# Two-layer graph attention: the place of the shared slot tile among the gathers of layer 2

## The chip, the core and the metric

The kernel runs on one core of a Trainium2 chip. The metric is the device time of one execution, in microseconds. A core has five engines with instruction queues of their own: TensorE (PE), VectorE (DVE), ScalarE (ACT), GpSimd (POOL) and SyncE (SP). SP, ACT and POOL also issue transfers between the chip's memory (DRAM) and the core's buffers; these run on 16 DMA engines that all queues share.

## The reference

The input is a graph of 3125 nodes with 768 features each, and 53,125 edges sorted by target node: 25,000 pairs in both directions and a loop on every node. The reference normalizes and rectifies the features, and passes them through two layers of graph attention:

```python
def gat_conv(x, edge_index, W, a_src, a_dst, bias, heads, out_ch, concat):
    xl = (x @ W).reshape(n, heads, out_ch)
    e = leaky_relu(alpha_src[src] + alpha_dst[dst], 0.2)
    e = exp(e - segment_max(e, dst)[dst])
    alpha = e / (segment_sum(e, dst)[dst] + 1e-16)
    out = segment_sum(xl[src] * alpha[:, :, None], dst)
...
h = relu(layer_norm(gat_conv(x, ei, W1, ..., 4, 256, True), g1, be1)) + (h0 @ Wr1 + br1)
h1 = h
h = layer_norm(gat_conv(h, ei, W2, ..., 1, 768, False), g2, be2) + (h1 @ Wr2 + br2)
return x + h
```

Layer 1 has four heads of 256 columns, layer 2 one head of 768. For every edge, the row of the edge's source node has to be fetched, weighted, and added into the row of its target node. `edge_index` adds one more loop per node, which the kernel treats apart (`own`).

## The kernel before

**Tiles.** The nodes are cut into 25 node tiles: 24 of 128 nodes and a last one of 53. The edges that end in a node tile are laid into 17 *slot tiles* of 128 slots each (`J = 17`, L31; 8 for the last node tile). A slot is one edge. The slot tiles belong to the four quarters of the node tile, 32 nodes each (`QUARTERS`); slot tile 0 belongs to the first quarter and slot tile 16 to the last. The node tiles form chains of three (`CHAIN = 3`): 0, 1, 2; then 3, 4, 5; and so on. Within a chain, slot tile 16 of one node tile and slot tile 0 of the next are the same tile: it holds the overhang of the first and the beginning of the second, and is gathered once. `shared(b)` says that node tile `b` has its slot tile 0 from the tile before: it is true for 1, 2, 4, 5, 7, 8 and so on up to 23.

**Layer 2.** `table2` in DRAM has one row of 784 numbers per node: 768 features, then the source score in column 768. A *gather* (`gather`, L206) fetches for one slot tile the 128 rows of its source nodes, some 400 KB, by an indirect transfer that GpSimd issues. Lines L210 and L214 are its two forms. L214 is used for the last slot tile of a node tile (16, or 7 in the last node tile) from the 37th gather on; it leaves out slots that hold no edge. The gathers of the whole layer are 400.

**The ring.** The gathered rows lie in a ring of 36 buffers `g0` to `g35` (`RING`, L1237). `slots_due` (L1333) is the list of all gathers in their order: node tile after node tile, and within one the five `ROUNDS` (0, 5, 9, 13), (1, 6, 10, 14), (4, 11, 15), (2, 8, 16), (3, 7, 12), less slot tile 0 where it is shared. Gather number n uses buffer n modulo 36. `fetch` (L1338) asks for further gathers as long as they are less than 36 ahead of the first one in the list whose rows are still needed (`unused`). A shared slot tile is still needed until the first round of the next node tile: `summed` lets it go there (L1408, L1409). A node tile takes 17 gathers, or 16 where its slot tile 0 is shared: 49 for a chain of three.

**Who uses a gathered tile.** Two engines do. ScalarE copies its score column into `slots` (`values`, L1357, L1360). When all slot tiles of a node tile have been copied, `softmax` (L1371) transposes the scores on TensorE into `mix` (L1378), takes maximum and exponentials, and transposes the weights back (L1394). Then `summed` (L1401) multiplies weights and rows on TensorE, one round at a time, into `pa` (L1421). `finish` (L1426) normalizes the node tile and stores it.

**The order.** The order of the instructions on TensorE, VectorE and ScalarE is the order in which the code writes them (`manual_schedule`, L1465). The main loop (L1482) goes through the node tiles b and their rounds. Rounds are counted from one in this text. In the second round the loop writes, behind `summed` and the square root of the finish of the tile before, the copies of the fourth round (slot tiles 2, 8, 16) of node tile b + 1; in the third round the copies of its fifth round (slot tiles 3, 7, 12) and the first half of its softmax; the second half and the steps of the residual product `pr` (`residuals`, helper line L190) fill the rest. So node tile b cannot go past its third round before all slot tiles of node tile b + 1 have landed.

The order on GpSimd and SyncE is not written by hand. A planner sets it when the kernel is built: it takes the instructions in the order of the code, but lets one that it holds ready pass an earlier one that is still waiting. An instruction that stands in GpSimd's queue runs in that order, and a gather waits there until the previous user of its buffer is done.

Of the kernel before, what the change touches and what calls it, by code (L numbers as in the profile page):

```python
# [30 lines left out]
J = 17  # L31
S = J * 128
QUARTERS = [(0,), (0,), (0,), (0,), (0, 1), (1,), (1,), (1,), (1, 2), (2,), (2,), (2,), (2, 3), (3,), (3,), (3,), (3,)]
ROUNDS = [(0, 5, 9, 13), (1, 6, 10, 14), (4, 11, 15), (2, 8, 16), (3, 7, 12)]
# [9 lines left out]
@with_exitstack  # L44
def preln_gat2_kernel(
    ctx: ExitStack,
    tc: tile.TileContext,
    x, src, dst,
    W1, a_src1, a_dst1, b1, g1, be1, Wr1, br1,
    W2, a_src2, a_dst2, b2, g2, be2, Wr2, br2,  # L50
    out,
):

    pool = ctx.enter_context(tc.tile_pool(name="flag", bufs=1))
    flag = pool.tile([1, 1], I32, name="flag")  # L60
    in_order(tc, x, src, dst, W1, a_src1, a_dst1, b1, g1, be1, Wr1, br1,
             W2, a_src2, a_dst2, b2, g2, be2, Wr2, br2, out, flag)
    other = tc.nc.values_load(flag[0:1, 0:1], min_val=0, max_val=1)
    with tc.If(other > 0):
        any_order(tc, x, src, dst, W1, a_src1, a_dst1, b1, g1, be1, Wr1, br1,
                  W2, a_src2, a_dst2, b2, g2, be2, Wr2, br2, out)
# [3 lines left out]
def in_order(  # L70
# [23 lines left out]
    NB = -(-N // P)  # L94
# [28 lines left out]
    def shared(b):  # L123

        return b < NB - 1 and b % CHAIN > 0
# [4 lines left out]
    def tiles_of(b):  # L130
        return J if b < NB - 1 else JL
# [1100 lines left out]
    with tc.tile_pool(name="m2", bufs=1, reuse_waits="tile") as mp, \  # L1232
# [95 lines left out]
        def filled(n):  # L1328
            for _ in range(n):
                next(fill, None)  # L1330

        gs = {}
        slots_due = [(b, j) for b in range(NB) for k in ROUNDS for j in k  # L1333
                     if j < tiles_of(b) and not (j == 0 and shared(b))]
        order_of = {s: i for i, s in enumerate(slots_due)}
        asked, unused = 0, set(range(len(slots_due)))

# [658 lines left out]
```

## Time and profile before

| | us |
|---|---|
| three runs | 1757.60, 1760.58, 1760.94 |
| median | 1760.58 |
| the profiled execution | 1760.3 |
| its span, first to last instruction | 1758.5 |
| mean granted TensorE clock | 0.968 |

The profile is that of one execution. In its lines a group or an instruction is named by its line in the kernel, its engine, its operation and the tiles that it writes and reads (`g<-table,idx_s` is a gather of the form L210, `g<-table,hi_s` one of L214). In the chain of waits each line has start, length and what the time went to. In the timeline each line has start, busy time, instruction, and in brackets the idle time of the engine before it, with what ended it. The windows have, for each stretch, its length, the busy time (and count) of PE, PEld (the loading of weights), DVE, ACT and POOL, the granted clock, the mean busy share of the DMA engines and the GB/s that they moved. The DMA share can come out slightly over 1.

### The profile page before, as it was taken

How to read it: one execution, taken by the hardware profiler on the slowest of the kernel's cores; microseconds unless marked ns; L12 is line 12 of the kernel's file. 1: busy time of each engine (PE TensorE's matmuls, PEld its weight loads, DVE VectorE, ACT ScalarE, POOL GpSimd, SP SyncE). 2: the span in 40 equal slices, each digit the busy share in tenths (PEclk: the TensorE clock that was granted, in tenths of full speed). 3: DMA queues.
4: the chain of work that ended last, by engine and by line, in shares of the span. 5: the costliest groups of instructions: out<-in, count | busy, mean ns of one | idle time of the engine just before them, and what ended most of it. 6: DMA issues, size and time to landing. Idle time of an engine off the chain costs nothing.

```text
span 1758.5 us, 31362 instructions
## 1 busy us (share of the span) xinstructions
PE 1632.8 (93%) x11522; PEld 936.7 (53%) x11522; DVE 1005.1 (57%) x2604; ACT 457.3 (26%) x1312; POOL 872.0 (50%) x908
## 2 busy tenths in 40 slices
PE   7999999999989999999999999997988988988984
PEld 5666666566656556556556555544444443443431
DVE  7784343788864566556565566641444544544545
ACT  2222342000122112212122122122333433433432
POOL 2000012100055766667666667627767667667662
PEclk9999999899989999999999999998999999989987
DMA  7833546533189999999999999969999999999994
GB/s 241 280 120 110 147 129 208 233 132 129 37 313 369 409 400 404 393 403 409 404 393 406 375 374 387 399 228 373 373 370 395 370 359 396 371 357 392 364 328 156
DMA packets 188644, 546.69 MB, mean 311 GB/s; under 512 B 32120, under 2 KB 80632, under 8 KB 188354
## 3 DMA queue, kind: packets, MB, share of 16 engines
q0 software_dynamic: 99632, 386.94, 57.9%
q1 hardware_dynamic: 84456, 147.27, 23.9%
q10 hardware_dynamic: 4394, 10.39, 1.5%
q8 instruction: 94, 1.54, 0.4%
q14 instruction: 68, 0.56, 0.1%
HBM read 492.19 MB, written 65.62 MB: 317 GB/s over the span
## 4 chain that ended last, share of the span: by engine, by line
PE 76%; DMA 14%; DVE 5%; issue 2%; ACT 2%; POOL 1%; SPq 0%; POOLq 0%; DVEq 0%; ACTq 0%
PE pr L190 18%; PE p L190 13%; PE pm L190 12%; PE pa L775 11%; PE pm L1027 7%; PE pa L1421 6%; DMA g<-table,idx_s 5%; DMA g<-table,hi_s 4%; PE pq L580 3%; PE mix L1378 1%; DMA w<-in_L_gnn_W_dram 1%; PE p L1190 1%; DMA h<-h1T_d 1%; DMA s<-slo_d 1%; PE pt L859 1%
## 5 line engine op out<-in xcount | busy, mean ns | idle before, releaser
L210 POOL DMA_INDIRECT g<-table,idx_s x393 | 378.8, 964 | 358.4 <-PE pq L610 170.9
L214 POOL DMA_INDIRECT g<-table,hi_s x423 | 433.6, 1025 | 203.8 <-issue 85.3
L190 PE MATMUL pr<-wr,h 128*128 128x384 f32 x768 | 277.3, 507 | 2.9 <-issue 2.1
L190 PE MATMUL p<-w,h1T 128*128 128x384 f32 (+1 forms) x768 | 267.7, 496 | 0.0
L775 PE MATMUL pa<-g,w 128*32 128x256 f32 x3912 | 246.7, 386 | 8.3 <-DVE w L752 5.6
L190 PEld LDWEIGHTS pr<-wr,h 128*128 128x128 f32 x768 | 143.7, 197 | 112.8 <-issue 35.9
L190 PEld LDWEIGHTS p<-w,h1T 128*128 128x128 f32 x768 | 139.8, 189 | 113.0 <-issue 21.4
L775 PEld LDWEIGHTS pa<-g,w 128*32 128x32 f32 x3912 | 119.7, 110 | 128.3 <-issue 23.8
L1421 PE MATMUL pa<-g,w 128*32 128x384 f32 x1956 | 176.7, 499 | 2.6 <-DVE v L1455 2.6
L752 DVE TENSOR_TENSOR w<-oh,al 128x128 f32<-128x128 f32 (+1 forms) x416 | 132.3, 318 | 51.9 <-PE pa L775 27.2
L190 PE MATMUL pr<-h0k,wr 128*128 128x256 f32 (+1 forms) x576 | 143.0, 395 | 2.5 <-DMA h0k<-h0T_d 2.5
L1027 PE MATMUL pm<-h0g,wr 128*128 128x512 f32 x288 | 133.1, 609 | 0.0
L190 PE MATMUL pm<-w,h0g 128*128 128x344 f32 x432 | 131.5, 459 | 0.3 <-ACT h0g L861 0.3
L190 PE MATMUL pm<-w,h0l 128*128 128x344 f32 x432 | 129.5, 454 | 0.0
L190 PEld LDWEIGHTS pr<-h0k,wr 128*128 128x128 f32 x576 | 106.9, 192 | 32.7 <-issue 10.7
L958 POOL DMA_DIRECT2D hot_d<-ohd x25 | 13.4, 535 | 213.2 <-DVE own L531 123.6
L1421 PEld LDWEIGHTS pa<-g,w 128*32 128x32 f32 x1956 | 57.5, 111 | 113.1 <-issue 104.7
L751 DVE TENSOR_SCALAR oh<-iota_f,rel_s 128x32 f32<-128x32 f32 (+1 forms) x416 | 114.4, 275 | 3.7 <-issue 3.5
L190 PEld LDWEIGHTS pm<-w,h0g 128*128 128x128 f32 x432 | 81.6, 193 | 40.1 <-issue 1.4
L190 PEld LDWEIGHTS pm<-w,h0l 128*128 128x128 f32 x432 | 80.5, 190 | 39.1 <-issue 0.2
L1382 DVE CUSTOM_DVE_ANT_0 mix<-mix,pen 128x640 f32<-128x640 f32 x25 | 20.8, 832 | 129.7 <-PE mix L1378 129.7
L1223 DVE COPY asad<-p 128x2 f32<-128x2 f32 (+1 forms) x25 | 4.0, 159 | 155.3 <-ACT row L1221 155.3
(295 smaller groups left out, 1751.4 us busy)
## 6 DMA issues: line engine op xcount, KB each, us to landing
s<-slo_d SPq DMA_DIRECT2D x25, 544.0 KB
table<-row SPq DMA_DIRECT2D x24, 512.0 KB
own<-table SPq DMA_DIRECT2D x24, 512.0 KB
h1T_d<-h1T SPq DMA_DIRECT2D x24, 512.0 KB
h<-h1T_d SPq DMA_DIRECT2D x88, 128.0 KB
table<-row SPq DMA_DIRECT2D x24, 392.0 KB
ring<-in_x_dram SPq DMA_DIRECT2D x24, 384.0 KB
out_dram<-z ACTq DMA_DIRECT2D x24, 384.0 KB
```

What stands on the lines that cost most here:

```text
L190: nc.tensor.matmul(out_, lhsT, rhs, start=start, stop=stop)
L210: nc.gpsimd.indirect_dma_start(out=g, out_offset=None, in_=table[:, :], in_offset=bass.IndirectOffsetOnAxis(ap=idx_s[:, c], axis=0))
L214: nc.gpsimd.indirect_dma_start(out=g, out_offset=None, in_=table[:, :], in_offset=bass.IndirectOffsetOnAxis(ap=idx_k[:, c], axis=0), bound ...
L580: nc.tensor.matmul(q[:, j], oh[:P, o:o + 128], tabs[:, i], start=(i == 0), stop=(i == 2))
L751: nc.vector.tensor_scalar(oh, iota_f[:, lo:hi], rel_s[:, c:c + 1], None, op0=OP.is_equal)
L752: nc.vector.tensor_tensor(w, oh[:, None, :].to_broadcast([128, heads, hi - lo]), al[:, POS[j], :, b:b + 1].to_broadcast([128, heads, hi - ...
L775: nc.tensor.matmul(pa[p0:p0 + 32, o // f, o % f:o % f + n], w[:, o // cols, :], g[:, o:o + n], start=to not in opened, stop=False, skip_gr ...
L859: nc.tensor.transpose(pt[:, k, :r], xt[:, (k0 + k) * 128:(k0 + k + 1) * 128], ident[:r, :r])
L1027: nc.tensor.matmul(pm, wr1[:, k, m * 128:(m + 1) * 128], groups[gi][:, k, :], start=(k == 0), stop=(k == NK1 - 1))
L1190: nc.tensor.transpose(pt[:, k, :r], z[:, (k0 + k) * 128:(k0 + k + 1) * 128], ident[:r, :r])
L1382: nc.vector.tensor_tensor_reduce(out=sums_, in0=sums_, in1=pen, scale=1.0, scalar=-BIG, op0=OP.add, op1=OP.max, accum_out=top)
L1421: nc.tensor.matmul(pa[p0:p0 + 32, i, :f], w_, g[:, i * f:(i + 1) * f], start=(i, q) not in opened, stop=False, skip_group_check=True)
```

## The change

In a node tile whose slot tile 16 is shared with the next one, that slot tile goes to the end of the node tile's gathers, behind slot tiles 3, 7 and 12. It was among the gathers of the fourth round. The order in which the rows are used, the copies on ScalarE and the matmuls stay as they are, and so does the order of gathers in node tiles whose slot tile 16 is not shared (2, 5, 8 and so on, 23 and 24).

```diff
         gs = {}
-        slots_due = [(b, j) for b in range(NB) for k in ROUNDS for j in k
-                     if j < tiles_of(b) and not (j == 0 and shared(b))]
+
+        def due(b):
+
+            js = [j for k in ROUNDS for j in k if j < tiles_of(b) and not (j == 0 and shared(b))]
+            return sorted(js, key=lambda j: j == J - 1) if shared(b + 1) else js
+
+        slots_due = [(b, j) for b in range(NB) for j in due(b)]
         order_of = {s: i for i, s in enumerate(slots_due)}
         asked, unused = 0, set(range(len(slots_due)))
```

## The prediction

> **What bounds the kernel now.** I read the page first, then the chain of waits in order of time, then windows and the timeline of layer 2. The edit touches only layer 2, which runs from about 1190 us to the end.
>
> ```profile
> PE 1632.8 (93%) x11522; PEld 936.7 (53%) x11522; DVE 1005.1 (57%) x2604; ACT 457.3 (26%) x1312; POOL 872.0 (50%) x908
> ...
> DMA  7833546533189999999999999969999999999994
> ...
> PE 76%; DMA 14%; DVE 5%; issue 2%; ACT 2%; POOL 1%; SPq 0%; POOLq 0%; DVEq 0%; ACTq 0%
> ```
>
> TensorE sets most of the chain, but 14% of it are transfers. The chain in order of time (start, length, what) says where, and they come in step:
>
> ```profile
> 1235.15 2.77 PE pa L1421 x32
> ...
> 1240.83 0.70 PE mix L1378 x5
> ...
> 1254.02 2.72 PE pa L1421 x32
> ...
> 1261.64 2.72 PE pa L1421 x32
> ...
> 1277.62 7.68 DMA g<-table,idx_s
> ...
> 1342.72 7.49 DMA g<-table,idx_s
> ...
> 1408.73 8.14 DMA g<-table,idx_s
> ...
> 1474.99 7.46 DMA g<-table,idx_s
> ...
> 1540.27 8.07 DMA g<-table,idx_s
> ...
> 1607.38 8.37 DMA g<-table,idx_s
> ...
> 1673.86 7.73 DMA g<-table,idx_s
> ...
> 1715.34 8.31 DMA g<-table,idx_s
> ```
>
> The first seven are some 66 us apart: one gather every three node tiles, in node tiles 2, 5, 8, 11, 14, 17 and 20, the last of each chain of three. (Node tile 0 starts at 1235.15 us, node tile 1 at 1254.02: an undisturbed one takes 18.8 us.) The eighth belongs to node tile 22. The timeline around the first, with idle time in brackets:
>
> ```profile
> 1276.37 0.95 POOL L210 DMA_INDIRECT g<-table,idx_s  x1 [0.30 <-issue]
> ...
> 1277.32 0.33 ACT L1360 ACTIVATE slots<-g 128x32 f32<-128x32 f32 x2
> ...
> 1277.62 0.95 POOL L210 DMA_INDIRECT g<-table,idx_s  x1 [0.30 <-ACT slots L1360]
> ...
> 1278.14 0.23 ACT L1360 ACTIVATE slots<-g 128x32 f32<-128x32 f32 x1 [0.49 <-DMA g<-table,hi_s]
> ...
> 1279.31 0.23 ACT L1360 ACTIVATE slots<-g 128x32 f32<-128x32 f32 x1 [0.94 <-DMA g<-table,idx_s]
> ...
> 1280.46 0.23 ACT L1360 ACTIVATE slots<-g 128x32 f32<-128x32 f32 x1 [0.93 <-DMA g<-table,idx_s]
> ...
> 1285.32 0.23 ACT L1360 ACTIVATE slots<-g 128x32 f32<-128x32 f32 x1 [4.63 <-DMA g<-table,idx_s]
> 1285.61 1.33 PE L1378 MATMUL mix<-ident,slots 128*128 128x128 f32 x5 [7.13 <-ACT slots L1360]
> ...
> 1302.44 0.94 POOL L210 DMA_INDIRECT g<-table,idx_s  x1 [3.71 <-PE pa L1421]
> ```
>
> ScalarE copies the score columns of node tile 3 in the order of the rounds: slot tiles 2 and 8 (the x2), 16 (the hi_s one), 3, 7, 12. The first three singles follow each other by 1.2 us; the last, slot tile 12, comes 4.9 us after its neighbour. TensorE stands 7.13 us for it. Slot tile 12 is the 69th gather of layer 2, counted on GpSimd:
>
> ```profile
> 1187.00:1278.60 91.60, 65.86 (x69) 0.93 1.01 374
> ```
>
> In the list of gathers it is the 66th (17 + 16 + 16 + 17, last of node tile 3). GpSimd's order is not written by hand, and the planner moved it. The program of the kernel before, as built, has at these places (place, node tile, slot tile, ring buffer):
>
> ```
> 64 (3, 7)  g28
> 65 (4, 5)  g30
> 66 (4, 9)  g31
> 67 (4, 13) g32
> 68 (3, 12) g29
> ```
>
> Buffer g29 held slot tile 16 of node tile 1, which node tile 2 reads too, in its first round; g30 to g32 held 3, 7 and 12 of node tile 1 and were free earlier. So three gathers of node tile 4 stand ahead of the one that everything waits for. The same swap stands at all seven places.
>
> **The change part by part.** No instruction is added or removed: 400 gathers before and after, the same bytes, the same matmuls in the same order. In 16 of 25 node tiles the shared slot tile goes from the 14th (13th) gather to the last, and 3, 7 and 12 move up by one.
>
> What it moves: a ring buffer is reused 36 gathers later, so the buffer that is held longest now comes up last of its node tile, where nothing stands behind it in that tile's list. The 66th gather is then slot tile 16 of node tile 3, into the buffer of slot tile 3 of node tile 1. That was read in the fifth round of node tile 1, the 2.72 us of rounds four and five at 1261.64, over by 1264.4; its turn on GpSimd comes about 1273.9. It does not wait, so the planner has no reason to let others pass.
>
> *First stall.* The last gather that node tile 3 needs is issued three places earlier: 3 x 1.25 us (starts 1276.37 and 1277.62) = 3.76 us. Against it: it is now slot tile 16, whose copy stands ahead of 3, 7 and 12 on ScalarE, so three copies follow the landing: 0.33 us for two less 0.21 for the first, 0.12 each, +0.36. Behind the waiting copy on ScalarE stand only those copies and the softmax that needs them; the square root of the tile before is issued ahead. Net **-3.4 us**. GpSimd passes no other queue, and SyncE's loads keep their order.
>
> *Each further three node tiles.* Here the gain is not 3.4 again: it is what the slower of GpSimd and the transfers leaves. The present period, landing to landing, is (1681.59 - 1285.30)/6 = 66.05 us. Windows (length, busy per engine, clock, DMA share, GB/s), then one of GpSimd without a pause and two of full transfers:
>
> ```profile
> 1285.30:1350.20 64.90, 57.96 (x366) 28.33 (x366) 30.85 (x57) 26.18 (x81) 46.59 (x49) 0.95 1.01 378
> 1350.20:1416.90 66.70, 58.00 (x366) 28.33 (x366) 30.84 (x57) 26.51 (x82) 47.34 (x50) 0.96 1.01 378
> 1416.90:1482.50 65.60, 58.72 (x366) 28.33 (x366) 30.84 (x57) 26.21 (x82) 46.13 (x49) 0.94 1.01 371
> 1482.50:1548.30 65.80, 58.44 (x366) 28.33 (x366) 30.84 (x57) 26.11 (x81) 47.26 (x50) 0.94 1.01 378
> 1548.30:1615.80 67.50, 59.56 (x366) 28.56 (x366) 30.86 (x57) 26.31 (x82) 47.26 (x50) 0.93 1.01 371
> 1615.80:1681.60 65.80, 58.28 (x366) 28.32 (x366) 30.88 (x57) 26.26 (x81) 45.99 (x50) 0.94 1.01 368
> 1681.60:1723.70 42.10, 33.48 (x272) 15.08 (x272) 20.83 (x39) 17.81 (x55) 28.40 (x30) 0.86 0.92 329
> ...
> 1237.00:1299.00 62.00, 54.87 (x343) 27.12 (x336) 24.84 (x48) 22.13 (x69) 46.74 (x49) 0.94 1.01 378
> 1327.00:1361.00 34.00, 27.05 (x168) 13.53 (x161) 14.11 (x24) 13.30 (x34) 25.77 (x28) 0.90 1.03 396
> 1515.00:1540.00 25.00, 24.04 (x163) 11.29 (x162) 13.91 (x26) 11.50 (x40) 19.05 (x20) 1.00 1.03 399
> ```
>
> GpSimd issues 49 gathers per period: 46.74 us of work and 49 pauses of 0.30 make 61.4 us. The transfers are length times GB/s, over the six rows 148.2 MB, 24.7 MB each; at 396 GB/s that is 62.4 us. TensorE needs 58 us of 65. So the floor is 62.4, set by the transfers, and the present 3.6 us above it are mostly GpSimd's pause of 3.71 us at 1302.44 (full ring): it waits for the first round of node tile 3, which the stall has put late.
>
> Does that pause go? From landing to that gather pass 1302.44 - 1285.32 = 17.1 us, with the copies 17.5. Between the new last gather (66th) and it (86th) lie 20 gathers, 20 x 1.25 = 25.1 us. The pause is gone if issue to landing takes 7.6 us or less; the seven above take 7.46 to 8.37, mean 7.85. A pause of about 0.2 us is left. Taking the floor and 0.4 us for this and for what the page cannot show of fuller queues, I put 62.8 us: 6 x 3.25 = **-19.5 us**. Bounds: 61.4 (GpSimd alone, -27.9) and 66.05 (0).
>
> *Tail.* From the seventh landing (1681.59) to the eighth (1723.65) pass 42.06 us, with two pauses of GpSimd:
>
> ```profile
> 1688.99 0.95 POOL L210 DMA_INDIRECT g<-table,idx_s  x1 [1.53 <-ACT pen L1366]
> ...
> 1700.18 0.94 POOL L210 DMA_INDIRECT g<-table,idx_s  x1 [3.94 <-PE pa L1421]
> ```
>
> After, 32 gathers lie between in place of 29: 40.2 us, and 0.5 for pauses that remain: **-1.4 us**. From the eighth landing on all is as now.
>
> Sum on the profiled execution: 1760.3 - 3.4 - 19.5 - 1.4 = **1736.0 us**. It stands 0.3 us under the median of the runs, which changes nothing.
>
> **The rivals.** *A slower landing (A).* If full queues raise issue to landing from 7.85 to 10 us, each period keeps a pause of 10 - 7.6 = 2.4 us: 61.4 + 2.4, about 64 us, 6 x 2.05 = 12.3 for 19.5: 1743. For it: the latency is already the tightest term. Against it: in the window from 1237 us GpSimd issued 49 gathers in 62 us without a pause, and a landing in it, 7.68 us, is no longer than the others. The 17.1 us also hold a slow restart: the five transposes at 1285.61 take 1.33 us after a wait of 7.13 us, those at 1240.83 without one 0.70 us. The Trainium skill, page "TensorE: Matmul & The Clock Gate", Part 1, says that an idle window of about 3.4 us halves the clock; the trace agrees (1.33 against 0.70 us), and by that rule shorter waits would shorten the 17.1 us and speak against this rival.
>
> *Transfers already full (B).* The DMA share is 1.01 in all windows, and if 374 GB/s were the most that this mix gives, three places on GpSimd would be queueing time only: 1760, no change. Against it: 396 and 399 GB/s over 34 and 25 us. The Trainium skill, page "DMA: Bandwidth & Descriptors", Specifications, puts the limit of HBM at about 358 GB/s for a core; by that 24.7 MB need 69 us and nothing can be won. The rows disagree.
>
> *The planner lets others pass again (C), slower.* If it sets gathers of node tile 4 ahead of slot tile 16, three of them give the old landing plus 0.36 us of copies, seven times: 1762.8, no change. From the fourth on each place costs 7 x 1.25 = 8.8 us; five: 1760.3 + 2.5 + 17.5 = 1780. For it: it did so before. Against it: it did so for a buffer that was held; this one is free 9.5 us earlier.
>
> **How the numbers follow.** Forecast 0.64, A 0.18, B 0.11 (with C's three places), C slower 0.07. About 0.2% (3.5 us) is what this measurement can tell from no change. Faster: forecast and A, 0.82; same 0.11; slower 0.07. The range: its lower end 1726 is GpSimd's 61.4 us (1760.3 - 3.4 - 27.9 - 1.4 = 1727.6) with a little less in the tail; its upper end 1755 takes in A and periods of 65.8 us. B and C lie outside.
>
> **What would show it.** Right: the swap is gone, node tile 3's last single copy in node tile 2 is the hi_s one with two or three copies close behind it; GpSimd's pauses of 3.5 to 3.9 us on the first round of node tiles 3, 6, 9 shrink below 1 us; the period is 62 to 63 us at 390 GB/s or more; TensorE's waits in node tiles 2, 5, 8 are some 3 us shorter, and new ones of about 1 us appear in the node tiles between. Wrong: pauses of GpSimd that stay (A), a period of 66 us with GB/s as now (B), a last landing at or behind 1285 us (C).

## The result

The changed kernel takes 1740.09 us (median of 4 runs, 1736.09 to 1742.46), the kernel before 1759.29 us beside it: a ratio of 0.989, 95% interval 0.9871 to 0.9909. The forecast was 1736.0 us. The profiled execution is the fastest of the four, 1736.09 us with a span of 1734.2 us, so the profile shows 24.2 us of gain and the medians 19.2.

The page of the kernel after, busy time and transfers in 40 slices. In the slices of layer 2 (it begins in the 28th) the DMA engines were busy for 90% and more before, and are again. In the six periods they moved 368 to 378 GB/s before; now it is 379 to 396, as the windows further down show:

```profile
PE 1631.4 (94%) x11522; PEld 934.8 (54%) x11522; DVE 1005.4 (58%) x2604; ACT 455.4 (26%) x1312; POOL 871.0 (50%) x908
...
DMA  7833546733179999999999999987999999999994
GB/s 243 281 116 114 151 129 184 270 128 116 50 270 376 407 404 395 403 387 408 407 398 405 377 384 378 410 332 263 381 391 383 395 394 394 396 394 396 381 356 164
```

No engine has other work than before. The timeline of the kernel after, around the first stall (start, length, engine, line, what; idle time before it in brackets):

```profile
1271.25 1.01 POOL L214 DMA_INDIRECT g<-table,hi_s  x1 [0.30 <-issue]
1272.57 0.96 POOL L210 DMA_INDIRECT g<-table,idx_s  x1 [0.30 <-issue]
...
1275.19 0.23 ACT L1365 ACTIVATE slots<-g 128x32 f32<-128x32 f32 x1 [0.22 <-DMA g<-table,idx_s]
...
1280.11 0.58 ACT L1365 ACTIVATE slots<-g 128x32 f32<-128x32 f32 x4 [4.68 <-DMA g<-table,hi_s]
...
1280.74 1.33 PE L1383 MATMUL mix<-ident,slots 128*128 128x128 f32 x5 [4.82 <-ACT slots L1365]
...
1298.59 0.95 POOL L210 DMA_INDIRECT g<-table,idx_s  x1 [2.43 <-PE pa L1426]
```

Slot tile 16 of node tile 3 (the hi_s gather at 1271.25) is now the 66th gather of layer 2, counted on GpSimd as in the list: nothing has passed it, and its pause is the usual 0.30 us. It lands at 1280.1, and its copy and those of 3, 7 and 12 run as one group of four. TensorE waits 4.82 us in place of 7.13. GpSimd's pause on the first round of node tile 3 is 2.43 us in place of 3.71.

The waits of the kernel before from 1240 to 1680 us (in total, how often, the longest), and then of the kernel after in the same stretch:

```profile
PEld mix L1378 <- ACT slots L1360: 57.5, 19, 8.4
...
ACT slots L1360 <- DMA g<-table,idx_s: 55.4, 37, 4.7
...
POOL g L210 <- PE pa L1421: 29.0, 22, 4.0
...
ACT slots L1360 <- DMA g<-table,hi_s: 3.1, 6, 0.8
```

```profile
PEld mix L1383 <- ACT slots L1365: 45.9, 20, 5.5
...
ACT slots L1365 <- DMA g<-table,hi_s: 29.1, 7, 5.0
...
POOL g L210 <- PE pa L1426: 16.8, 26, 2.4
...
ACT slots L1365 <- DMA g<-table,idx_s: 15.5, 20, 2.0
```

ScalarE now waits for the hi_s gather and no longer for the last idx_s one, and for both together 44.6 us in place of 58.5. GpSimd's waits for a buffer, less 0.30 us for each, fall from 22.4 to 9.0 us.

Windows of the kernel after, from one last landing to the next (length, busy per engine, clock, DMA share, GB/s):

```profile
1280.10:1342.70 62.60, 58.98 (x366) 28.39 (x366) 30.88 (x57) 25.84 (x81) 45.85 (x49) 0.95 1.02 387
1342.70:1405.70 63.00, 58.25 (x366) 27.88 (x366) 30.87 (x57) 26.25 (x81) 46.73 (x50) 0.97 1.03 394
1405.70:1468.80 63.10, 59.39 (x366) 28.50 (x366) 30.86 (x57) 25.84 (x81) 46.79 (x50) 0.95 1.03 394
1468.80:1531.30 62.50, 58.25 (x366) 27.79 (x366) 30.86 (x57) 25.93 (x81) 46.93 (x50) 0.97 1.03 395
1531.30:1594.70 63.40, 58.08 (x366) 28.33 (x366) 30.90 (x57) 26.17 (x82) 47.76 (x51) 0.97 1.03 396
1594.70:1659.00 64.30, 58.27 (x366) 27.66 (x366) 30.88 (x57) 26.16 (x81) 46.16 (x49) 0.96 1.03 379
1659.00:1698.90 39.90, 33.02 (x272) 14.94 (x272) 20.84 (x39) 18.00 (x57) 28.70 (x30) 0.88 0.99 360
```

The period is (1659.0 - 1280.1)/6 = 63.15 us, was 66.05. GpSimd's turns in it are 46 of 1.25 us and 3 hi_s ones of 1.32 (1271.25 to 1272.57), 61.6 us. The difference of the two profiled executions comes apart so: layer 2 starts 1.8 us earlier (first gather at 1185.89, was 1187.73; ahead of it the change does nothing), the landing that ends the first stall comes another 3.4 us earlier, the six periods give 17.4 us and the tail 2.2 (39.9 in place of 42.06), and some 0.5 us are lost behind the last landing.

### The profile page after: what moved, and what is told of

Same layout as the page of the kernel before. It is cut to its first block, busy times and chain, and to the rows that moved or that the text cites. A ratio compares the mean times of both kernels' runs of the same rounds, so it can differ in the third digit from the quotient of the medians.

```text
span 1734.2 us, 31366 instructions
## 1 busy us (share of the span) xinstructions
PE 1631.4 (94%) x11522; PEld 934.8 (54%) x11522; DVE 1005.4 (58%) x2604; ACT 455.4 (26%) x1312; POOL 871.0 (50%) x908
## 3 DMA queue, kind: packets, MB, share of 16 engines
q1 hardware_dynamic: 84456, 147.27, 24.3%
## 5 line engine op out<-in xcount | busy, mean ns | idle before, releaser
L775 PEld LDWEIGHTS pa<-g,w 128*32 128x32 f32 x3912 | 119.7, 110 | 129.1 <-issue 24.2
L520 ACT ACTIVATE bn_sd<-bn_mv,eps 128x1 f32<-128x1 f32 (+1 forms) x50 | 14.7, 295 | 276.9 <-DVE bn_mv L516 272.2
```

The source lines that it names most:

```text
L520: nc.scalar.activation(sd, mv[:, 1:2], AF.Sqrt, bias=eps[:P])
L775: nc.tensor.matmul(pa[p0:p0 + 32, o // f, o % f:o % f + n], w[:, o // cols, :], g[:, o:o + n], start=to not in opened, stop=False, skip_gr ...
```

## The experiments

Theory: the gain is the three places on GpSimd that the planner's swap takes from the last gather of node tiles 3, 6, 9, ..., and from then on GpSimd's turns or the transfers set the period. Rival: any moved boundary frees ring buffers earlier, and that is the gain. For what sets the period after the change, three candidates: GpSimd's turns (G), full transfers (T), the loop of the ring (L).

**Only the second boundary of each chain.**

```
-            return sorted(...) if shared(b + 1) else js
+            return sorted(...) if shared(b + 1) and b % CHAIN == 1 else js
```

> Only the boundaries behind node tiles 1, 4, 7, ... are moved (slot tile 16 last there); behind node tiles 0, 3, 6, ... the list is that of before. Theory (the gain is the three places that the planner's swap costs the last gather of node tiles 3, 6, ...): the buffer of slot tile 16 of node tile 1 comes up at place 68 and holds nothing, so the last gather of node tile 3 (slot tile 12, place 65) is in its turn; no copies stand behind it. The whole gain, 1736 to 1741 us, up to 2.5 us under the changed kernel. Rival (any of the moved boundaries frees ring buffers a round earlier for three gathers, and this is the gain): half of it, about 1750 us.

1735.67 us, ratio 0.9869 (0.985 to 0.9888): the whole gain with half of the moves. Its period is 63.13 us. That it lies under the changed kernel (0.989) is not settled: the intervals overlap, and the two did not run beside each other. Its waits from 1240 to 1680 us show that the hi_s gather is nobody's last any more:

```profile
PEld mix L1383 <- ACT slots L1365: 45.9, 21, 5.6
ACT slots L1365 <- DMA g<-table,idx_s: 36.5, 36, 1.6
...
ACT slots L1365 <- DMA g<-table,hi_s: 4.0, 6, 1.1
```

**Only the first boundary of each chain.** The same line with b % CHAIN == 0.

> Only the boundaries behind node tiles 0, 3, 6, ... are moved. Slot tile 16 of node tile 1 stays at place 29, so place 65, now slot tile 16 of node tile 3, meets its held buffer: it is issued at place 68 again, three gathers of node tile 4 ahead of it and 3, 7 and 12 too. Theory: the last landing of node tile 3 is as late as before, plus three copies on ScalarE (0.36 us, seven times): 1759 to 1763 us, no gain, and GpSimd's pauses of 3.5 to 3.9 us on the first round of node tiles 3, 6, ... stay. Rival (each moved boundary counts): about 1750 us.

1760.15 us, ratio 1.0012 (0.9999 to 1.0024): nothing of the gain. The rival falls. Its timeline and, in a second fence, its waits from 1240 to 1680 us:

```profile
1275.50 1.01 POOL L214 DMA_INDIRECT g<-table,hi_s  x1 [0.30 <-ACT bn_sd L520]
...
1282.47 0.58 ACT L1365 ACTIVATE slots<-g 128x32 f32<-128x32 f32 x4 [6.82 <-DMA g<-table,hi_s]
...
1283.11 1.33 PE L1383 MATMUL mix<-ident,slots 128*128 128x128 f32 x5 [6.63 <-ACT slots L1365]
```

```profile
PEld mix L1383 <- ACT slots L1365: 58.0, 19, 8.0
ACT slots L1365 <- DMA g<-table,hi_s: 42.7, 6, 7.5
...
POOL g L210 <- PE pa L1426: 32.9, 29, 4.0
```

The shared slot tile of node tile 3 meets the held buffer and is issued 89.2 us behind the first gather of layer 2 (1275.50 less 1186.31); before, slot tile 12 was issued 89.9 us behind it. It is the 69th gather on GpSimd and the 66th of its list: three gathers of node tile 4 have passed it, as they passed slot tile 12 before. Which slot tile is last doesn't matter; its place does.

**GpSimd's order by hand, nothing moved.** The list of before, with the planner's swaps taken out:

```
-        with tc.manual_schedule(engines={PE, ACT, DVE}):
+        with tc.manual_schedule(engines={PE, ACT, DVE, POOL}):
```

> The list of before, no slot tile moved; GpSimd's order in layer 2 is that of the list, the planner may not let gathers pass. Slot tile 12 of node tile 3 is at place 65 and waits for the first round of node tile 2, which is over at about the time of its turn (1273.6 against 1273.9 us in the profile of before). Theory: the same gain as the changed kernel without moving anything, 1735 to 1741 us, the period between last landings 62.5 to 63.5 us. Rival (the list of before needs the passing, since the held buffers of places 49 and 65 stop GpSimd itself): pauses of GpSimd of 1 us or more at slot tile 0 and slot tile 12 of node tiles 3, 6, ..., and 1750 to 1760 us.

1750.72 us, ratio 0.9957 (0.9944 to 0.997): 8 of the 19 us. Theory and rival are both half right. The 66th gather, slot tile 12 of node tile 3, goes out in its turn with the usual pause. But there are two held buffers in each chain, and the planner had let gathers pass at both. The other one is at the 50th gather, slot tile 0 of node tile 3; its buffer is held until the first round of node tile 1. In the profile of before the 50th gather starts at 1253.73 us after the usual pause, ahead of that round (1254.02), so it was another one. GpSimd's timeline in this kernel at that gather, and 49 gathers later:

```profile
1251.37 0.95 POOL L210 DMA_INDIRECT g<-table,idx_s  x1 [0.30 <-ACT w L1398]
1255.07 0.95 POOL L210 DMA_INDIRECT g<-table,idx_s  x1 [2.75 <-issue]
...
1315.73 0.95 POOL L210 DMA_INDIRECT g<-table,idx_s  x1 [0.30 <-ACT w L1398]
1319.39 0.94 POOL L210 DMA_INDIRECT g<-table,idx_s  x1 [2.71 <-issue]
```

In order, GpSimd itself stands there in each period, 2.2 us on average beyond the usual pause (1.3 to 2.5). Windows of this kernel between last landings, the first and the last of six:

```profile
1283.00:1347.50 64.50, 58.45 (x366) 28.34 (x366) 30.84 (x57) 26.58 (x82) 46.98 (x50) 0.95 1.01 382
...
1607.10:1672.00 64.90, 58.40 (x366) 28.30 (x366) 30.85 (x57) 26.60 (x81) 46.56 (x49) 0.95 1.01 373
```

The period is (1672.0 - 1283.0)/6 = 64.8 us: 61.6 of turns, 2.2 at that gather, the rest smaller pauses. So the planner's first swap was worth keeping (the gather that it puts off is the first of node tile 3, not the last that its softmax waits for, and the kernel with the second boundaries, which leaves this one as it was, has the whole gain) and its second one cost three places where everything waits. The change moves both buffers out of the way.

**The copy of slot tile 16 behind the others.** On top of the change, in the score copies:

```
-            for j in ROUNDS[k]:
+            late = shared(b + 1)
+            js = [j for j in ROUNDS[k] if not (late and j == J - 1)]
+            for j in js + [J - 1] * (late and k == len(ROUNDS) - 1):
```

> The changed kernel, and on ScalarE the score copy of slot tile 16 also goes behind those of 3, 7 and 12 where its gather is the last. Theory: the three copies that now follow the last landing (0.36 us) are gone from the chain at the seven stalls, and each is part of the loop from landing to the first round of the next node tile, to buffers free, to the next gathers: 7 x 0.36 = 2.5 us, about 1737.5 us. Rival (GpSimd's places or the transfers set the period, the landing only the first stall): 0 to 0.4 us, 1740 us.

1734.84 us, ratio 0.987 (0.9852 to 0.9887). Undecided: the median is 5 us under that of the changed kernel, more than the theory asked for, but the intervals overlap and the two did not run beside each other. The profile shows the saving, but not in the period. From the last landing to the first gather that waits for the next first round pass 17.2 us on average in place of 18.1, and TensorE's waits ahead of the transposes in node tiles 5, 8, 11, 14 and 17 fall from 3.4 to 4.1 us to 0 to 1.8. Yet the period is 63.5 us, not shorter: the last gathers take 8.7 us from issue to landing in place of 8.3, waits of up to 2.9 us appear in other node tiles, and TensorE stands idle for 33.3 us in all from 1240 to 1680 us, for 32.5. The first stall ends earlier, 4.0 us counted from the first gather of layer 2: 1.3 us by the issue (GpSimd's pause at the first reuse of the ring was 1.20 us in this execution, 3.08 in the changed kernel's, which the copies don't explain), 1.0 by a quicker landing, and 1.6 because four of the five transposes no longer wait for slot tile 16.

**Dose and traffic, on other chips.** Four kernels went to a chip on which the kernel before takes 1923.97 us, and two more to one on which it takes 1955.60. Each is the changed kernel with one edit:

```
two fills        + if k in (1, 3): nc.gpsimd.memset(room, 0.0)
more traffic     + if k == 0: nc.sync.dma_start(spare_d[:, :], shares[b][0])
less traffic     + if b > 2 and b < NB: h1s[b] = kept[1 + b % 2]      (no load)
two additions    + if k in (1, 3): nc.gpsimd.tensor_tensor(room, room, room, OP.add)
35 buffers       - RING = 36
                 + RING = 35
```

> The changed kernel and two fills of a small unused tile on GpSimd in each node tile (second and fourth round), between gathers: six per three node tiles, 0.2 to 0.4 us each by the fill of 128x128 elements in the profile of before (0.20 us), so 1.2 to 2.4 us of GpSimd per period of 63.1 us. Theory G (GpSimd's 49 turns of 1.26 us and its remaining pauses set the period): all of it comes out, 8 to 16 us over the changed kernel, 1748 to 1756 us. Theory T (the transfers at 394 to 396 GB/s set it, GpSimd has 1.3 us to spare in a period): 0 to 5 us, 1740 to 1745 us, and GpSimd's remaining pauses shrink by as much as the fills take.

> The changed kernel and one further transfer per node tile, the 128x640 weights written to an unused place in memory, 0.33 MB, 0.98 MB per three node tiles beside 24.8 MB. Theory T (396 GB/s is the ceiling): 25.8 MB need 65.1 us per period in place of 63.15, about 14 us more, 1754 us. Theory G (the ceiling is higher, 396 GB/s is only what the gathers ask for): the windows show 405 to 410 GB/s, and 0 to 4 us more, 1740 to 1744 us.

> The changed kernel, whose loads of h1 are left out from node tile 3 on (the residual product runs on the first tiles in their place, so this product is of other rows): 0.52 MB less per node tile, 1.57 MB of 24.8 per three node tiles. Theory T: 23.2 MB at 396 GB/s are 58.7 us, so GpSimd's 61.7 us take over: 1.4 us per period, about 10 us less, 1730 us, at 378 GB/s. Theory G: the period keeps GpSimd's 61.7 us; its pauses (1.4 us per period) are the wait for the ring, and they shrink only as far as issue to landing gets shorter than the 7.5 us mean of now; between 0 and 10 us less, with shorter landings.

> The changed kernel itself, for the same chip and the same runs of before: 1736 to 1742 us. It says whether the kernels with only the second boundaries moved (1735.7) and with the copy of slot tile 16 behind (1734.8) are really faster than it.

> The changed kernel and one addition on a small unused tile (128x224) on GpSimd in the second and the fourth round of each node tile, six per three node tiles. By the 1.83 us of the 53x768 addition at the end it takes 0.53 us; some 0.15 us of it can lie in the 0.30 us pause ahead of the next gather (the fill of 0.31 us moved the next gather by 0.17 us only), so 0.38 us each, 2.3 us per period of 63.15 us. Theory G (GpSimd's 61.7 us of turns and its 1.4 us of remaining pauses add up, nothing else sets the period): 2.3 us per period, about 17 us over the changed kernel, ratio to before 0.998. Theory T (the transfers set it and the pauses are only what GpSimd is let off): 61.7 + 2.3 = 64.0 in place of 63.15, 6 us, ratio 0.992.

> The changed kernel with 35 ring buffers in place of 36. Theory L (the remaining pauses are the loop of the ring: last landing, softmax, first round, buffers free, next gather, and it has no slack): the pause on the first round of node tiles 3, 6, ... is one turn of GpSimd longer, 1.26 us per period, about 9 us over the changed kernel, ratio 0.994, and pauses of 1.5 to 3.5 us there. Theory T (the transfers set the period): fewer gathers in flight only make the queues shorter, 0 to 3 us, ratio 0.989 to 0.991, and landings that are shorter by up to 1.2 us.

First chip: fills 0.9953 (0.9926 to 0.998), more traffic 0.9979 (0.9957 to 1.0001), less traffic 0.9956 (0.9931 to 0.9981), the change itself 0.9967 (0.9944 to 0.9989). Second chip: additions 0.9936 (0.9915 to 0.9957), 35 buffers 0.9966 (0.994 to 0.9992). Nothing can be told apart, and the change is worth 0.3% in place of 1.1%. The page of the changed kernel on the first of these chips, with its first windows between the same landings in a second fence:

```profile
DMA  7823548331899999999999997858888989899884
GB/s 237 291 93 128 138 136 304 120 123 49 317 374 358 376 405 384 393 383 398 358 386 377 373 377 270 289 212 301 308 298 296 311 298 317 288 310 308 298 264 134
```

```profile
1341.00:1423.20 82.20, 69.30 (x371) 31.67 (x367) 31.04 (x57) 25.51 (x81) 46.73 (x50) 0.90 0.89 300
1423.20:1505.60 82.40, 66.08 (x370) 30.58 (x366) 30.94 (x57) 25.51 (x81) 46.74 (x50) 0.88 0.89 301
```

In layer 1 (12th to 24th slice) the transfers are a little slower than above, 358 to 405 GB/s; in layer 2 they run at 300, with a DMA share of 0.89. But it is not they that set the period there. TensorE's waits on this chip from 1340 to 1840 us, and then, for the same kernel on the chip of the result, from 1240 to 1680 us ("issue" is time in which it waited for nothing that the profile shows):

```profile
PE pr L190 <- issue: 49.3, 47, 2.2
...
PE pa L1426 <- issue: 18.0, 33, 1.6
```

```profile
PE mix L1383 <- ACT slots L1365: 32.5, 12, 4.9
```

On the slow chip TensorE doesn't wait for a score copy once in six periods. It stands some 11 us in each between single matmuls, for no reason that the profile shows, and is busy for nearly all of the rest. The gathers land sooner than above, 5.2 us after their issue on average for 7.5. GpSimd has 61.7 us of turns and 20.2 us of pauses in a period of 81.9 us (six periods, from issue to issue of the last gather), and most of that is waiting for TensorE to free a buffer. The last gather is not what is waited for there, and so three places, or a dose, hardly count.

**The additions again, on a chip with 1759.73 us before.**

> The kernel with one addition of 128x224 on GpSimd in the second and the fourth round of each node tile once more, because on the chip of the last runs the kernel before takes 1956 us and GpSimd pauses 20 us per period, so that nothing of the two theories can be seen there. Where the kernel before takes about 1760 us: theory G (turns and pauses of GpSimd add up) 17 us over the changed kernel, ratio to before 0.998; theory T (transfers set the period, GpSimd's 1.5 us of pauses take the dose in) 6 us, ratio 0.992. Where it takes over 1900 us again: GpSimd has 20 us per period to spare and the ratio is that of the changed kernel, 0.994 to 0.997.

1745.99 us, ratio 0.9919 (0.9905 to 0.9933), where theory T gave 0.992 and theory G 0.998. GpSimd's timeline of this kernel at one addition, and in further fences its waits from 1240 to 1680 us and two windows:

```profile
1349.88 0.95 POOL L210 DMA_INDIRECT g<-table,idx_s  x1 [0.30 <-ACT v L1396]
1350.85 0.57 POOL L1501 TENSOR_TENSOR room<-room 128x224 f32<-128x224 f32 x1
1351.57 0.95 POOL L210 DMA_INDIRECT g<-table,idx_s  x1 [0.16 <-DMA g<-table,idx_s]
1352.83 0.95 POOL L210 DMA_INDIRECT g<-table,idx_s  x1 [0.30 <-DMA g<-table,idx_s]
```

```profile
POOL g L210 <- PE pa L1427: 4.3, 15, 0.3
```

```profile
1283.00:1347.00 64.00, 59.52 (x368) 28.78 (x367) 31.16 (x59) 26.27 (x82) 49.98 (x55) 0.95 1.03 387
1347.00:1411.00 64.00, 57.21 (x365) 27.67 (x365) 29.95 (x55) 25.95 (x81) 49.62 (x56) 0.98 1.02 384
```

One addition moves the next gather by 1.69 - 1.25 = 0.44 us, six by 2.6 us per period. The period grows only from 63.15 to 64.3 us, taken from issue to issue of the last gather (64.5 from landing to landing), which is 61.6 + 2.6 and next to nothing more: every pause of GpSimd for a buffer is gone (15 waits for `pa`, none over the usual 0.3 us), and the rate falls from some 394 to 385 GB/s. Mean time from issue to landing from 1240 to 1680 us falls from 7.5 to 6.9 us. So in the changed kernel GpSimd's turns fill all but 1.5 us of a period, and a dose uses up these 1.5 us first. That theory T gave the right ratio doesn't show that the transfers made the pauses: any other cause of the same 1.5 us would give it too.

**35 buffers again, on a chip with 1755.63 us before.**

> The changed kernel with 35 ring buffers once more, for a chip on which the kernel before takes about 1760 us. Theory L (the 1.5 us of pauses per period that are left are the loop of the ring, from last landing by softmax and first round to the next free buffer, and nothing is queued that could give way): one turn more of pause, 1.26 us per period, about 9 us over the changed kernel, ratio 0.994, period 64.4 us. Theory T (at 394 GB/s the transfers are full, and landings are as long as the number of gathers in flight makes them): landings shorter by up to 1.2 us from 7.5 us, period 63.2 to 63.5 us, ratio 0.989 to 0.991. Where the kernel before takes over 1900 us: longer pauses in both cases, and only the ratio to before is of use.

1741.17 us, ratio 0.9915 (0.9885 to 0.9944): the interval holds both theories. The profiled execution, slowest of its four runs, has a period of 64.45 us, and its waits from 1240 to 1680 us have 13.1 us of pauses (less 0.30 each) for 9.0:

```profile
POOL g L210 <- PE pa L1426: 20.9, 26, 3.0
```

From issue to issue the period is 64.3 us, 1.1 over that of the changed kernel where L gave 1.26, and the pauses have grown by the same 1.1. That speaks for L; landings of 7.1 us on average in place of 7.5 speak for T. The kernel with the copy of slot tile 16 behind the others speaks against L: there the way from the last landing to the next free buffer was 0.9 us shorter, and the period was not. And layer 1 of the changed kernel moved 401 GB/s from 700 to 900 us, in packets of other sizes, so 394 to 396 GB/s is not the most that these engines move whatever they carry. Whether the last 1.5 us are the ring's or the transfers' stays open.

## Why the prediction was right, and where its sizes were off

*The mechanism* was right: the swap is gone, and the three places are the gain. The pair of half changes shows it, since the half that leaves slot tile 16 of node tile 1 in its place gains nothing. What the prediction didn't see is that only half of the edit is needed, and that the planner's other swap, at the 50th gather, did no harm: taking both swaps out without moving a slot tile gives only 8 us.

*First stall*, -3.4 us: TensorE restarts 3.0 us earlier, counted from the first gather of layer 2, and the landing comes 3.4 earlier where 3.76 were forecast. That both are close is in part luck. The last gather goes out 4.5 us earlier, of which the three places are 3.76 and most of the rest pauses ahead of them that were shorter in this execution; and it takes 8.83 us to land in place of 7.68. The copies cost 0.63 us from landing to TensorE's start in place of 0.29, so +0.34 for the +0.36 of the prediction.

*Each further three node tiles*, 62.8 us: measured 63.15 in the fastest run, so 17.4 us for 19.5. This is the term that was mis-sized, in the direction of rival A and by some 30% of the way. The pause on the first round of node tiles 3, 6, 9, ... was to be 0.2 us and below 1 us at the most; it was 2.43, 0.49, 1.67, 0.57, 0.70 and 1.81, three of six above, 1.0 us on average beyond the usual 0.30. Two readings are behind it. From issue to landing the seven last gathers took 7.67 to 9.34 us, mean 8.3, for 7.85. And from landing to the first new gather pass 17.6 to 18.8 us, mean 18.1, where 17.5 were taken over: the prediction read 17.1 off the first stall, the second shortest of seven. In the kernel before they are 17.1 to 18.7 us, mean 17.8, and with 0.36 for the copies that is the 18.1.

*The sum.* 1736.0 us was forecast, and the profiled execution took 1736.09. That it fits so well is luck: 1.8 us of its gain lie ahead of layer 2, where the change does nothing, and make up for most of what the periods lack. By the medians the change is worth 19.2 us, not 24.3. The median lies 4 us over the profiled execution, and no profile shows in which term the other runs lose that.

*The floor*: 62.4 us by transfers and 61.4 by GpSimd. The rate of 394 to 396 GB/s, in four of the six periods, is where it was expected. But the additions show that GpSimd has less than 2.6 us to spare, so the two floors lie within 2% of each other. The period is GpSimd's 61.6 us of turns and 1.5 of pauses; what makes the pauses stays open.

*Tail*, -1.4 us: measured -2.2.

*Rivals.* B (transfers already full) fell where the kernel before takes 1760 us: 394 GB/s against 374. The limit of about 358 GB/s per core in the Trainium skill, page "DMA: Bandwidth & Descriptors", Specifications, is passed in all six periods. On the slow chip where the change alone ran it brings 0.3%, but not for B's reason: TensorE doesn't wait for gathers there. C (gathers pass again) did not come in the changed kernel; it came in the kernel with the first boundaries alone, where three gathers of node tile 4 stand ahead of slot tile 16. For three, C gave the old time plus the copies, 1762.8 us for 1760.3; measured are 1760.15 for 1758.89.

*TensorE's restart.* The prediction said of the Trainium skill's rule on the clock gate (page "TensorE: Matmul & The Clock Gate", Part 1) that shorter waits would shorten the 17.1 us. They did not (18.1 us on average, 0.36 of it copies, for 17.8 before). TensorE's waits in the seven stalls are 3.4 to 4.9 us, for 6.5 to 7.7, still at the rule's 3.4 or over it. Behind four of them the five transposes still take 1.33 us. Behind the other three they take 0.77 to 0.89, but there the matmuls that follow are slow: the granted clock in the 7 us or so behind the landing is 0.59 to 0.79 in all seven.

## What to carry to other kernels

When a planner orders a DMA-issuing engine, compare its list with the built order at every buffer that is held longer than the others: a pass is free where the passed gather has time left, and costs a place each where it is the last one that a softmax or a reduction waits for. A stall that comes back once per chain gives its places in full only in the first chain; from the second on, the next bound sets what is left of them (here 2.9 us of 3.76), so work out the turns of the issuing engine and the bytes before counting the gain seven times. Where a wait comes back in every chain, read it in all of them and not in the first alone. And try each half of a two-part move alone.

## What was not expected of the hardware

The same program takes 1756 to 1760 us on three of the chips here and 1924 and 1956 us on two others. On the one with 1924 us, 158 of the 187 us between the spans of the changed kernel lie in layer 2 (its first gather is at 1214.96 us, for 1185.89). There TensorE stands between single matmuls, with a granted clock of 0.88 to 0.90 in the windows above for 0.95 to 0.97, and the transfers run at 300 GB/s for 394. In the records of single transfers (1240 to 1680 us) the packets of 6,272 bytes take about the same in the middle, 239 ns on the slow chip and 249 on the other, but the slowest twentieth takes over 0.62 us there and over 0.27 here. A gather has landed when its last packet has. Why these packets are slow, why TensorE stands, and whether the two hang together was not tried, and what else ran on these chips at the time is not on record.

The pause of 0.30 us between two gathers on GpSimd is not lost to other work. GpSimd's timeline of the kernel with the fills:

```profile
1399.25 0.96 POOL L210 DMA_INDIRECT g<-table,idx_s  x1 [0.31 <-issue]
1400.19 0.32 POOL L1500 MEMSET room<- 128x224 f32 x1
1400.67 0.95 POOL L210 DMA_INDIRECT g<-table,idx_s  x1 [0.16 <-issue]
```

The fill starts at once and the next gather comes 1.42 us after the one before in place of 1.26: 0.16 us for 0.32 us of work. In the additions 0.44 us for 0.57, so about 0.15 us of each fits into the pause.
